# Two hT blocks per load and an earlier preparation of the last group, in a gated graph layer on one core

## The chip, the cores and the metric

The kernel runs on one core of one Trainium2 chip. The metric is the device time of one execution in microseconds. Four executions of the kernel before took 1185.64 to 1194.97 us, median 1188.67.

## What is computed

For 16 graphs (batch b) of 1024 nodes with 256 features x, with one sparse weighted adjacency matrix `adj` (1024 x 1024, shared by the batch):

```
pre_u  = x @ W1[:256]             pre_v = x @ W1[256:]
S[u,v] = sigmoid( sum_k relu(pre_u[u,k] + pre_v[v,k] + b1[k]) * W2[k] + b2 )
a[v]   = sum_u S[u,v] * adj[u,v] * x[u]
m[v]   = (sum_u adj[u,v] * x[u]) * x[v]
out    = beta1*x + beta2*(a @ Wa + ba) + beta3*(m @ Wm + bm)
```

S matters only where adj is not zero, so the kernel works on lists of edges.

## The kernel before

**Units of work.** The batch is cut into `NG` = 4 groups of `GB` = 4 graphs, the nodes v into `NT` = 8 blocks of 128. A pair (group, node block) is one unit `k`, 32 in all, in the sequence `order` (L381): group 0 blocks 0 to 5, group 1 blocks 0 to 5, group 0 blocks 6 and 7, group 1 blocks 6 and 7 (these last four are `again`, L382), then groups 2 and 3 whole. A unit takes 10 steps (`T`), so there are 320 steps; step `n` belongs to unit `n // 10` and has a place `s = n % 10` in it. Below, "block 180" means steps 180 to 189. The main loop is L700 to L778. Every engine works through its instructions in the order in which the program writes them (`manual_schedule`, L444), so the order is written out by hand.

**One step.** GpSimd gathers (L469, `fetch`) 128 rows of 8 KB, 1 MB, from a table in DRAM: each row holds pre_u and x of one neighbour u for the four graphs. There are five buffers, and the gather for step n + 4 is issued in step n, after the aggregation of step n - 1 has freed its buffer. VectorE adds pre_v to the gathered pre_u (L555, one instruction, "the gating add"), then does relu, times W2 and the sum for each graph (L559, four times). ScalarE takes the sigmoid (L562) and scales the left operand (L565). TensorE aggregates (L576) in the step after and spreads pre_v for the step after next to the edges (`expand`, L539), into one of two PSUM buffers.

**Beside the steps, by s.** At s = 0 and 2 TensorE computes pre_v of the next unit (`halves`, L425; w_v in L400). At s = 1, 7, 9 results are transposed (L594). At s = 3 to 6 `block_end` multiplies by Wa and Wm (L625) for the unit before; its result z leaves by a 512 KB store (L631), and at s = 0 the block of x that goes into it is loaded (h_blk, L730), both on SP's queue. VectorE multiplies by x in `times_h` (L607), which reads hT; for the second half of unit k that is at step 10k + 13, and then hT of the unit is dropped (L609). In steps 0 to 107 the edge lists of node blocks 4 to 7 are made as well (`advance`, L675), with GpSimd fetching two columns of edge values per step.

**Preparing the tables.** Each table row block needs two things: a copy of x from DRAM to DRAM (`copy_h`, L392, 512 KB, on ScalarE's queue in the main loop), and pre_u, computed from hT, the transposed x block of 128 partitions x 8 x 128 numbers (`load_hT`, L386: 512 KB, in runs of 512 bytes, on SP's queue). `rows` (L407) computes pre_u in two pieces of 8 matmuls (w_u in L400), each copied out by ScalarE (L416); one step after the second piece the result is stored in the table (L419) by SP. All of a group's table must be in place before its first gather, which is issued four steps ahead of the group's first step: steps 56, 156 and 236 for groups 1, 2 and 3. hT is read again by `halves` and by `times_h` when the unit itself is processed. For the four units in `again` it is dropped after `rows` and loaded a second time.

**When.** Group 0 is prepared ahead of the main loop ("the lead"; the order is the script at L488, the loads are at L478 to L483). For the others, `plan` (L681) gives each block the step of its load and copy and the steps of its two row pieces (L687 to L692). Each load is put at the end of its step (L765).

**Buffers.** The pool `hts` (L213) has NT + 2 = 10 buffers of one block each, `hta` (L214) three for the `again` units. A load into a buffer waits, on SP's queue, until the last reader of the block that had the buffer before is done. The last unit's output rows use one more tile of `hts` (L732).

Of the kernel before, what the change touches and what calls it, by code (L numbers as in the profile page):

```python
# [7 lines left out]
FP = mybir.dt.float32  # L8
# [5 lines left out]
P = 128  # L14
# [3 lines left out]
def kernel(  # L18
# [42 lines left out]
    nc = tc.nc  # L61
    B, N, D = x.shape
    NT = N // P
    DC = D // P
    GB = 4
    NG = B // GB
# [20 lines left out]
    xT_rows = xT.rearrange("b (c p) n -> p (b c) n", p=P)  # L87
# [121 lines left out]
    main = ctx.enter_context(ExitStack())  # L209
    gat = main.enter_context(tc.tile_pool(name="gat", bufs=1))  # L210
    one = main.enter_context(tc.tile_pool(name="one", bufs=1))
    big = main.enter_context(tc.tile_pool(name="big", bufs=2))
    hts = main.enter_context(tc.tile_pool(name="hts", bufs=NT + 2))  # L213
    hta = main.enter_context(tc.tile_pool(name="hta", bufs=3))  # L214
    wk = main.enter_context(tc.tile_pool(name="wk", bufs=3))
    psc = main.enter_context(tc.tile_pool(name="psc", bufs=2, space=bass.MemoryType.PSUM))
# [157 lines left out]
    def after(step, f):  # L374
        due.setdefault(step, []).append(f)
# [5 lines left out]
    order = [(g, vt) for some in (range(FIRST), range(FIRST, NT)) for g in range(2) for vt in some]  # L381
    again = [(g, vt) for g, vt in order if vt >= FIRST]  # L382
    order += [(g, vt) for g in range(2, NG) for vt in range(NT)]
    hTs = {}

    def load_hT(k):  # L386
        g, nt = k
        hTs[k] = hta.tile([P, GB, DC, P], FP, name="hT_") if k in again else hts.tile([P, GB, DC, P], FP, name="hT")
        nc.sync.dma_start(hTs[k].rearrange("p b c n -> p (b c) n"),
                          xT_rows[:, g * GB * DC:(g + 1) * GB * DC, nt * P:(nt + 1) * P])  # L390

    def copy_h(k, engine=nc.scalar):  # L392
        g, nt = k
# [53 lines left out]
    def do(step):  # L447
        for f in due.pop(step, ()):
            f()
# [10 lines left out]
    BS = NG * NT  # L460
# [15 lines left out]
    turn = [(g, vt) for g in range(2) for vt in (*range(FIRST, NT), *range(FIRST))]  # L476
    tabs = [fetched[0][:, :GD], *(f[:, GD:] for f in fetched)]
    for i in range(NT):  # L478
        if i < 2:
            next(made[i])  # L480
        load_hT(turn[i])
        if i in (5, 7):
            next(made[i // 2])  # L483
    COPIES = 2
# [5 lines left out]
    m = 0  # L490
# [76 lines left out]
    def aggregate(n):  # L567
        k, g, vt, w, j = where(n)
        left, f = lefts.pop(n), fetched[n % NF]
        for i, q in enumerate(QUARTERS[j]):  # L570
            h, r = divmod(q, 2)
            first = j == h * MID and r == 0
            if first:
                accs[h] = psa.tile([P, 2, D], FP, name=f"acc{h}")
            for b in range(GB):
                nc.tensor.matmul(accs[h][b * 2 * V:(b + 1) * 2 * V, r, :],  # L576
                                 left[:, i, b].rearrange("p k v -> p (k v)"), f[:, GD + b * D:GD + (b + 1) * D],
                                 start=first, stop=(j == q + 1), skip_group_check=True)


    def half_end(n, q):

        evs[q] = one.tile([P, 2, D], FP, name=f"ev{q}")
        nc.scalar.copy(evs[q], accs.pop(q))  # L584
# [94 lines left out]
    loads, at = {}, {}  # L679

    def plan(blocks, ns):  # L681

        for k, (load, *pieces) in zip(blocks, ns):
            loads[load] = k
            at.update((n, k) for n in pieces)

    plan(turn[NT:], ((0, 5, 8), (6, 12, 15), (12, 18, 22), (17, 25, 28), (24, 32, 35), (31, 38, 42), (38, 45, 48),  # L687
                     (43, 50, 52)))
    plan([(2, vt) for vt in range(NT)], ((60 + 10 * i, 68 + 10 * i, 71 + 10 * i) for i in range(NT)))
    plan([(3, vt) for vt in range(NT)], ((141, 149, 151), (149, 158, 161), *((153 + 10 * i, 161 + 10 * i, 168 + 10 * i)  # L690
                                                                             for i in range(2, NT - 1)), (223, 231, 234)))
    plan(again, ((103,), (113,), (125,), (133,)))  # L692
    begun = set(turn[:NT])
    end = parts = piece = last = None
    load_mark(0)
    for n in range(2):
# [3 lines left out]
    for n in range(total + 2):  # L700
        k, s = divmod(n, T)
        if 1 <= n <= total:
            aggregate(n - 1)
            fetch_val(2)
            if n - 1 + NF < total:
                fetch(n - 1 + NF)
            if n % TW in (0, MID + 1):
                half_end(n - 1, 0 if n % TW else 1)
        if n < total:
            gate(n)  # L710
            if n + 1 < total:
                left_adj(n + 1)
        if n % TW == 1 and n // TW + 1 < total // TW:
            load_mark(n // TW + 1)
        do(n)
        if n + 2 < total:
            expand(n + 2)
        if n == 1:
            w_a = load_weights(Wa, "w_a", nc.sync)
            w_m = load_weights(Wm, "w_m", nc.sync)  # L720
            bias = load_rows(bm, D, "bias", nc.sync)
            ba_b = load_rows(ba, D, "ba_b", nc.sync)
            be1 = load_rows(beta1, 1, "be1", nc.sync)
            be2 = load_rows(beta2, 1, "be2", nc.sync)
            be3 = load_rows(beta3, 1, "be3", nc.sync)
            after(10, scale_late)
        if s == 0 and 0 < k < BS:
            hbs[k - 1] = big.tile([P, GB, D], FP, name="h_blk", bufs=1)
            g, vt = order[k - 1]
            nc.sync.dma_start(hbs[k - 1], x_rows[vt * P:(vt + 1) * P, g * GB:(g + 1) * GB, :])  # L730
        if n == total - 6:
            hbs[BS - 1] = hts.tile([P, GB, DC, P], FP, name="hT").rearrange("p b c n -> p b (c n)")  # L732
            for v, m, f in tails:
                for h, o in tail_rows(x, v, m, f):
                    nc.sync.dma_start(h, o)
        for i in advance.get(n, ()):
            next(made[i], None)
        if (s == 1 and 0 < k < BS) or n == total:
            turn_over(k - 1, 1, 1, n)
        if s in (3, 4, 5, 6) and 0 < k < BS:  # L740
            if s == 3:
                end = block_end(k - 1)
                next(end)
            go(end, n)
        if s == 7 and k < BS:
            turn_over(k, 0, 0, n)
            turn_over(k, 0, 1, n)
# [12 lines left out]
        if k + 1 < BS and s in (0, 2, 3, 5, 6):  # L760
            if s == 0:
                parts = halves(k + 1)
                next(parts)
            go(parts, n)
        if n in loads:  # L765
            load_hT(loads[n])
            if loads[n] not in begun:
                copy_h(loads[n])
                begun.add(loads[n])
        if n in at:  # L770
            if at[n] != last:
                last = at[n]
                piece = rows(last)
                next(piece)
            go(piece, n)
        if n == 100:
            nc.gpsimd.partition_all_reduce(longest, rest, P, bass_isa.ReduceOp.max)
            after(n + 12, count_rest)  # L778
# [7 lines left out]
    with tc.If(any_left > 0):  # L786
        with ExitStack() as s2:
# [3 lines left out]
            for vt in range(NT):  # L791
# [3 lines left out]
                for b in range(B):  # L795
                    hT = fw.tile([P, DC, P], FP, name="fb_hT")
# [96 lines left out]
```

## Time and profile before

| | us |
|---|---|
| median of four runs | 1188.67 |
| the profiled execution, its own time | 1181.59 |
| its span, first to last instruction | 1179.7 |
| first gating add (step 0) starts at | 71.16 |
| first gating add of group 1 (step 60) | 310.7 |
| first gating add of group 2 (step 160) | 653.8 |
| first gating add of group 3 (step 240) | 909.6 |
| last gating add (step 319) | 1159.1 |

The profile is of one execution. In it "PE" is TensorE's matmuls and "PEld" its weight loads, which overlap them, DVE is VectorE, ACT ScalarE, POOL GpSimd, SP SyncE, whose only work is to issue DMAs. A matmul's end is modelled, so a PE that is busy all the time is not PE at its peak. "A <- B" in a list of waits means that A stood idle until B ended; "remote" is a release that the profile can't attribute. The trace also has a record of every DMA packet: queue q0 is GpSimd's, q1 is SP's, q10 is ScalarE's. A share of 1.00 is 16 DMA engines busy; since packets overlap, up to 1.17 is seen in the lead.

### The profile page before, as it was taken

Reading aid. Unit: us, or ns where it says so; the run is one execution under the profiler, and the core shown is the slowest. Engines: PE = TensorE matmul, PEld = TensorE weight load, DVE = VectorE, ACT = ScalarE, POOL = GpSimd, SP = SyncE. Lnnn points to the kernel's source line nnn. Section 1 sums busy time; section 2 is a strip of 40 time slices with the busy share of each in tenths; the row PEclk is TensorE's granted clock in tenths of the full one; section 3 lists DMA queues with packets and bytes.
Section 4 is the critical chain, followed back from the end, with each engine's and each line's share of the span. In section 5 each row is a group of like instructions: output and inputs, shape, how many; then the busy total and the mean of one; then the engine's idle time right before and its main releaser. Section 6 shows DMA issues by size and latency. Waiting matters only on the chain. (4 is left out here: it accounts for less than half of the span.)

```text
span 1179.7 us, 23919 instructions
## 1 busy us (share of the span) xinstructions
PE 1095.8 (93%) x7633; PEld 726.6 (62%) x7633; DVE 1063.1 (90%) x3487; ACT 893.5 (76%) x2624; POOL 437.5 (37%) x428
## 2 busy tenths in 40 slices
PE   7767899999799999999999999999999999999986
PEld 6644566666566666566666666666666566666653
DVE  7678789979998999899999999999999999999994
ACT  2437577778678886788887888888888888888873
POOL 1546663343253332633332333333333333333330
PEclk9968999999999999999999999999999999999999
DMA  9987799999989998999999999999999999999992
GB/s 283 303 284 237 254 339 372 315 318 383 319 268 350 366 382 302 308 379 380 385 380 364 363 354 350 370 371 366 380 358 341 351 319 323 329 332 335 325 352 82
DMA packets 147047, 391.40 MB, mean 332 GB/s; under 512 B 16752, under 2 KB 105328, under 8 KB 110704
## 3 DMA queue, kind: packets, MB, share of 16 engines
q0 software_dynamic: 50016, 300.50, 69.7%
q1 hardware_dynamic: 81616, 74.99, 19.7%
q10 hardware_dynamic: 15280, 14.29, 3.7%
q8 instruction: 63, 1.03, 0.3%
q14 instruction: 72, 0.59, 0.1%
HBM read 393.78 MB, written 50.33 MB: 376 GB/s over the span
## 5 line engine op out<-in xcount | busy, mean ns | idle before, releaser
L469 POOL DMA_INDIRECT fetched<-table,uidx x320 | 340.3, 1064 | 647.8 <-PE acc L576 498.1
L559 DVE SCALAR_TENSOR_TENSOR t<-t,w_b 128x256 f32<-128x256 f32 x1280 | 469.6, 422 | 22.5 <-ACT left L565 0.5
L555 DVE TENSOR_TENSOR t<-fetched,pc 128x1024 f32<-128x1024 f32 x320 | 389.4, 1217 | 47.3 <-DMA fetched<-table,uidx 17.9
L576 PE MATMUL acc<-fetched,left 128*32 128x256 f32 x4096 | 340.4, 391 | 36.3 <-ACT left L565 24.4
L565 ACT ACTIVATE left<-left,gt 128x32 f32<-128x32 f32 (+1 forms) x1280 | 299.3, 304 | 10.4
L539 PE MATMUL pc<-X,mark 128*128 128x512 f32 x640 | 236.9, 452 | 13.8 <-DVE t L555 8.9
L576 PEld LDWEIGHTS acc<-fetched,left 128*32 128x32 f32 x4096 | 134.7, 109 | 184.4 <-issue 56.6
L539 PEld LDWEIGHTS pc<-X,mark 128*128 128x128 f32 x640 | 96.8, 190 | 147.6 <-issue 78.8
L562 ACT ACTIVATE gt<-sc,b_b 128x4 f32<-128x4 f32 x320 | 96.2, 301 | 74.0 <-DVE t L559 68.8
L625 PE MATMUL misc<-w_m,LT 128*128 128x256 f32 x496 | 117.2, 379 | 0.0
L625 PE MATMUL misc<-w_a,LT 128*128 128x256 f32 x496 | 117.1, 379 | 0.0
L549 ACT ACTIVATE left<-onehot,val 128x128 f32<-128x128 bf16 (+1 forms) x320 | 116.5, 364 | 0.0
L400 PE MATMUL misc<-w_u,hT 128*128 128x256 f32 x448 | 107.8, 387 | 5.1 <-ACT few L310 3.6
L400 PE MATMUL misc<-w_v,hT 128*128 128x256 f32 x448 | 108.8, 387 | 0.0
L559 DVE DVE_READ_ACCUMULATOR t<-t,w_b 128x1 f32 x1280 | 104.4, 82 | 0.0
L625 PEld LDWEIGHTS misc<-w_a,LT 128*128 128x128 f32 x496 | 93.9, 189 | 15.0
L625 PEld LDWEIGHTS misc<-w_m,LT 128*128 128x128 f32 x496 | 93.9, 189 | 15.0
L357 POOL DMA_INDIRECT val<-in_adjT_dram,vidx x80 | 84.4, 1055 | 32.7 <-issue 23.6
L400 PEld LDWEIGHTS misc<-w_v,hT 128*128 128x128 f32 x448 | 87.3, 195 | 14.4
L400 PEld LDWEIGHTS misc<-w_u,hT 128*128 128x128 f32 x448 | 84.8, 193 | 16.9 <-ACT few L310 3.7
L597 ACT COPY LT<-misc 128x512 f32<-128x512 f32 x128 | 70.2, 573 | 19.3 <-PE pc L539 7.6
L584 ACT COPY ev<-acc 128x512 f32<-128x512 f32 x128 | 75.6, 591 | 11.0 <-PE acc L576 3.7
(161 smaller groups left out, 895.1 us busy)
## 6 DMA issues: line engine op xcount, KB each, us to landing
h_blk<-in_x_dram SPq DMA_DIRECT2D x31, 512.0 KB
out_dram<-z SPq DMA_DIRECT2D x31, 512.0 KB
hT<-in_xT_dram SPq DMA_DIRECT2D x28, 512.0 KB
table<-tab SPq DMA_DIRECT2D x26, 512.0 KB
table<-in_x_dram ACTq DMA_DIRECT2D x24, 512.0 KB
fetched<-table,uidx POOLq DMA_INDIRECT x320
table<-in_x_dram SPq DMA_DIRECT2D x8, 512.0 KB
table<-fetched SPq DMA_DIRECT2D x6, 512.0 KB
```

The source lines that it names most:

```text
L357: nc.gpsimd.indirect_dma_start(out=val[:, i, j:j + 1], out_offset=None, in_=adj_flat, in_offset=bass.IndirectOffsetOnAxis(ap=vidx[:, i, j: ...
L400: nc.tensor.matmul(p[:, bb * D:(bb + 1) * D], hT[:, 2 * h + bb, i, :], wt[:, i, :], start=(i == 0 and not begun), stop=(i == DC - 1), skip ...
L469: nc.gpsimd.indirect_dma_start(out=fetched[n % NF], out_offset=None, in_=table[g], in_offset=bass.IndirectOffsetOnAxis(ap=uidx[:, vt * NW ...
L539: nc.tensor.matmul(pcs[n][:, c], marks[n // TW][:, j * P:(j + 1) * P], cuts[k][:, w, c], start=True, stop=True)
L549: nc.scalar.activation(lefts[n][:, :m, :, 0, :], onehot[:, i, o:o + m, :].unsqueeze(2).to_broadcast([P, m, GB, V]), AF.Copy, scale=val[:, ...
L555: nc.vector.tensor_tensor(t, fetched[n % NF][:, :GD].rearrange("p (b d) -> p b d", b=GB), pcs.pop(n).rearrange("p (b d) -> p b d", b=GB), ...
L559: nc.vector.scalar_tensor_tensor(t[:, b, :], t[:, b, :], 0.0, w2_b, ALU.max, ALU.mult, accum_out=sc[:, b:b + 1])
L562: nc.scalar.activation(gt, sc, AF.Sigmoid, bias=b2_b)
L565: nc.scalar.activation(lefts[n][:, :m, b, 1, :], lefts[n][:, :m, b, 0, :], AF.Copy, scale=gt[:, b:b + 1])
L576: nc.tensor.matmul(accs[h][b * 2 * V:(b + 1) * 2 * V, r, :], left[:, i, b].rearrange("p k v -> p (k v)"), f[:, GD + b * D:GD + (b + 1) * D ...
L584: nc.scalar.copy(evs[q], accs.pop(q))
L625: nc.tensor.matmul(pz[:, bb * D:(bb + 1) * D], LTs[k][:, c, 2 * h + bb, i, :], wt[:, c, :], start=False, stop=(i == 0 and c == DC - 1), sk ...
```

## The change

`load_hT` loads two neighbouring node blocks of a group at once into one tile of twice the width, so that the runs are 1024 bytes; `hts` has 5 such tiles in place of 10 single ones. The call for the second block of a pair then finds it there and loads nothing. Blocks 2, 3 and 4 of group 3 (`alone`) are loaded by themselves into `hta`, as are the four loads of `again`; block 7 of group 3 has no partner left and goes alone into a wide tile. The very first pair is loaded as two halves (`apart`). The steps in `plan` are new for groups 1 to 3, the copy is issued ahead of the load in a step, and the last output tile comes from `hta`.

```diff
-    hts = main.enter_context(tc.tile_pool(name="hts", bufs=NT + 2))
+    hts = main.enter_context(tc.tile_pool(name="hts", bufs=NT // 2 + 1))
...
-    def load_hT(k):
+    alone = [(NG - 1, vt) for vt in range(2, 5)]
+    def load_hT(k, apart=False):
         g, nt = k
-        hTs[k] = hta.tile([P, GB, DC, P], FP, name="hT_") if k in again else hts.tile([P, GB, DC, P], FP, name="hT")
-        nc.sync.dma_start(hTs[k].rearrange("p b c n -> p (b c) n"),
-                          xT_rows[:, g * GB * DC:(g + 1) * GB * DC, nt * P:(nt + 1) * P])
+        blocks = [k]
+        if k in begun or k in alone:
+            t = hta.tile([P, GB, DC, P], FP, name="hT_")
+        else:
+            t = hts.tile([P, GB, DC, 2 * P], FP, name="hT")
+            if nt + 1 < NT:
+                blocks.append((g, nt + 1))
+        n = P * len(blocks)
+        for c in range(0, n, P) if apart else (0,):
+            m = P if apart else n
+            nc.sync.dma_start(t.rearrange("p b c n -> p (b c) n")[:, :, c:c + m],
+                              xT_rows[:, g * GB * DC:(g + 1) * GB * DC, nt * P + c:nt * P + c + m])
+        for i, k in enumerate(blocks):
+            hTs[k] = t[:, :, :, i * P:(i + 1) * P]
+            begun.add(k)
...
-        load_hT(turn[i])
+        if i % 2 == 0:
+            load_hT(turn[i], i == 0)
...
-    plan(turn[NT:], ((0, 5, 8), (6, 12, 15), (12, 18, 22), (17, 25, 28), (24, 32, 35), (31, 38, 42), (38, 45, 48),
-                     (43, 50, 52)))
-    plan([(2, vt) for vt in range(NT)], ((60 + 10 * i, 68 + 10 * i, 71 + 10 * i) for i in range(NT)))
-    plan([(3, vt) for vt in range(NT)], ((141, 149, 151), (149, 158, 161), *((153 + 10 * i, 161 + 10 * i, 168 + 10 * i)
-                                                                             for i in range(2, NT - 1)), (223, 231, 234)))
+    plan(turn[NT:], ((0, 8, 11), (5, 12, 15), (7, 18, 21), (12, 23, 25), (24, 32, 35), (31, 38, 41), (44, 51, 52),
+                     (46, 53, 54)))
+    plan([(2, vt) for vt in range(NT)], ((64, 72, 73), *((60 + 10 * i, 68 + 10 * i, 71 + 10 * i) for i in range(1, NT))))
+    plan([(3, vt) for vt in range(NT)], ((131, 148, 151), (139, 158, 161), (158, 168, 171), (163, 178, 181),
+                                         (170, 188, 191), (183, 194, 198), (188, 202, 208), (203, 214, 218)))
...
-            hbs[BS - 1] = hts.tile([P, GB, DC, P], FP, name="hT").rearrange("p b c n -> p b (c n)")
+            hbs[BS - 1] = hta.tile([P, GB, DC, P], FP, name="hT_").rearrange("p b c n -> p b (c n)")
...
         if n in loads:
-            load_hT(loads[n])
-            if loads[n] not in begun:
+            if loads[n] not in copied:
                 copy_h(loads[n])
-                begun.add(loads[n])
+                copied.add(loads[n])
+            if loads[n] not in hTs:
+                load_hT(loads[n])
```

`turn[NT:]` is group 1 in the sequence of blocks 6, 7, 0, 1, 2, 3, 4, 5. With the pairs, group 1 is loaded in steps 0, 7, 24, 44, group 2 in 64, 80, 100, 120, group 3 in 131, 158, 163, 170, 183, 203.

More of the change, by code (lines that the diff above doesn't have):

```diff
@@ L383 @@
     order += [(g, vt) for g in range(2, NG) for vt in range(NT)]
-    hTs = {}
-    def load_hT(k):
+    hTs, begun = {}, set()
+    alone = [(NG - 1, vt) for vt in range(2, 5)]
+    def load_hT(k, apart=False):
         g, nt = k
-        hTs[k] = hta.tile([P, GB, DC, P], FP, name="hT_") if k in again else hts.tile([P, GB, DC, P], FP, name="hT")
-        nc.sync.dma_start(hTs[k].rearrange("p b c n -> p (b c) n"),
-                          xT_rows[:, g * GB * DC:(g + 1) * GB * DC, nt * P:(nt + 1) * P])
+        blocks = [k]
[13 more added lines that the diff above has]
+            begun.add(k)
     def copy_h(k, engine=nc.scalar):
@@ L685, in plan @@
             at.update((n, k) for n in pieces)
-    plan(turn[NT:], ((0, 5, 8), (6, 12, 15), (12, 18, 22), (17, 25, 28), (24, 32, 35), (31, 38, 42), (38, 45, 48),
-                     (43, 50, 52)))
-    plan([(2, vt) for vt in range(NT)], ((60 + 10 * i, 68 + 10 * i, 71 + 10 * i) for i in range(NT)))
-    plan([(3, vt) for vt in range(NT)], ((141, 149, 151), (149, 158, 161), *((153 + 10 * i, 161 + 10 * i, 168 + 10 * i)
-                                                                             for i in range(2, NT - 1)), (223, 231, 234)))
+    plan(turn[NT:], ((0, 8, 11), (5, 12, 15), (7, 18, 21), (12, 23, 25), (24, 32, 35), (31, 38, 41), (44, 51, 52),
[3 more added lines that the diff above has]
+                                         (170, 188, 191), (183, 194, 198), (188, 202, 208), (203, 214, 218)))
     plan(again, ((103,), (113,), (125,), (133,)))
-    begun = set(turn[:NT])
+    copied = set(turn[:NT])
     end = parts = piece = last = None
```

## Prediction

> **What bounds the kernel now.** I read the page first (shares by engine, DMA by slice), then the busy time block by block (ten steps each, cut at the start of every tenth gating add, L555), then what the VectorE waits for, then the DMA packets of three short windows.
>
> ```profile
> PE 1095.8 (93%) x7633; PEld 726.6 (62%) x7633; DVE 1063.1 (90%) x3487; ACT 893.5 (76%) x2624; POOL 437.5 (37%) x428
> ...
> DMA  9987799999989998999999999999999999999992
> ```
>
> TensorE, VectorE and the DMA engines are all near full, so no single row names the bound; the blocks do. Columns: stretch, length, then busy us (and instructions) of PE, PEld, DVE, ACT, POOL, clock, DMA share, GB/s.
>
> ```profile
> 232.30:272.00 39.70, 37.35 (x260) 24.73 (x259) 30.36 (x97) 28.86 (x85) 18.64 (x20) 1.00 0.93 339
> 346.90:382.80 35.90, 33.32 (x230) 21.93 (x229) 30.31 (x96) 28.03 (x84) 15.36 (x16) 1.00 0.99 349
> 717.40:748.80 31.40, 31.40 (x229) 20.86 (x227) 30.25 (x97) 26.85 (x81) 10.16 (x10) 1.00 0.98 344
> 780.70:813.50 32.80, 32.80 (x242) 21.60 (x235) 30.21 (x97) 27.84 (x84) 11.72 (x11) 1.00 1.00 371
> 877.10:909.60 32.50, 31.94 (x229) 21.32 (x229) 30.25 (x97) 27.34 (x81) 11.26 (x10) 1.00 0.94 346
> 909.60:942.50 32.90, 31.78 (x233) 20.13 (x225) 30.26 (x97) 26.64 (x81) 11.11 (x11) 1.00 0.98 360
> 973.80:1005.10 31.30, 30.15 (x217) 19.20 (x216) 30.15 (x97) 26.32 (x80) 10.50 (x11) 1.00 0.91 326
> ```
>
> The last line is a block of the last group (steps 260 to 269), with nothing prepared beside it: VectorE works 30.15 us of 31.30. That is the floor of a block. Blocks 180, 200 and 230 (third to fifth line) carry two row pieces each: PE is busy nearly all the time and DMA is at 0.94 to 1.00, three limits within a few per cent of each other. Block 240 has no pieces and is still 1.6 us over. The first two lines (steps 40 to 49, 70 to 79) have the same VectorE work and are 4.6 to 8.4 us longer: these are real stalls. Their causes, VectorE alone, steps 0 to 79 and then 80 to 249:
>
> ```profile
> DVE t L555 <- DMA fetched<-table,uidx: 6.7, 4, 2.8
> DVE t L555 <- PE pc L539: 6.5, 4, 2.0
> DVE t L555 <- remote: 6.0, 4, 2.4
> ```
>
> ```profile
> DVE t L555 <- DMA fetched<-table,uidx: 10.1, 17, 1.5
> DVE t L555 <- PE pc L539: 3.9, 6, 1.1
> ```
>
> In all some 19 us early and 14 us later are waits for a gather or for PE. A change that only moves loads and pieces can't win more, and can lose by adding to them.
>
> **What the Trainium skill says.** (1) "DMA: Bandwidth & Descriptors", section "Why small descriptors are slow (HBM only)": each packet carries a fixed overhead. The trace agrees. In three windows (12 to 18 us: only hT loads, 512 B packets; 62 to 72 us: 8 KB gathers beside hT; 973.8 to 1005.1 us: 1 KB packets of h_blk and z):
>
> ```profile
> q1 hardware_dynamic: 3440, 1.74, 116.2%
> ```
>
> ```profile
> q0 software_dynamic: 570, 3.89, 93.6%
> q1 hardware_dynamic: 526, 0.26, 9.0%
> ```
>
> ```profile
> q1 hardware_dynamic: 1014, 1.00, 9.4%
> ```
>
> Share x window x 16 / packets gives 32.4 ns and 27.4 ns for 512 B, 46.5 ns for 1 KB. (2) Same page, "Queues, rings and completion order": each DMA engine takes turns between queues packet by packet. The second window agrees: 570 gather packets beside 526 hT packets. So a gather of 8 KB packets keeps most of an engine, and a burst on SP's queue delays gathers modestly but for long. (3) Same page, "Issuing engines are not separate DMA queues": that copy_h stays on ACT's queue doesn't take it out of the same sum.
>
> **The change, part by part.**
>
> *Pairs.* 32 first loads become 13 pair loads and 6 singles (the first pair is sent as two). A pair costs 1024 x 46.5/16 = 2.98 us of DMA time against 2048 x 27.4/16 = 3.51 (or 4.15 at 32.4 ns): 0.5 to 1.2 us less, 0.7 taken, as the mean of all 36,864 packets of 512 B in the trace is 29 ns. 13 x 0.7 = 9 us of DMA time, most of it where DMA doesn't set the end. Matmuls (L400) and the product (L607) have the same shapes: nothing. SP issues 13 loads fewer; worth nothing, as SP mostly waits. The same SBUF is used (5 x 8 KB against 10 x 4 KB a partition).
>
> *Lead (0 to 71 us).* Three pairs save 2 us of DMA before the copies. But the first gating add waits for PE at 71.16, behind the list chain of VectorE that ended in ACT few L310 at 68.5, not for a gather (the first is issued at 56.2). Cover: that chain. Value 0; range -1.7 (all of it shows) to +1 (blocks 0 and 1 of group 0 land together: first used at 17.3 us, and their 1 MB is in by about 15 by the packet count).
>
> *Steps 0 to 79.* Loads of group 1 and 2 move from 0, 6, 12, 17, 24, 31, 38, 43, 60, 70 to 0, 7, 24, 44, 64, so none lies on step 70 any more, where h_blk, z, a copy and hT met and the gather of step 74 was 2.81 us late: -2.0 taken, 0 to -2.8. Each new wait is for a pair buffer; by the code its last reader is the product L607 of step 23, 43, 63, one step ahead of the load on SP, and what is queued behind the load is later work. Price 0. Row pieces at 42 and 45 go (to 41, 51): the one at 42 ran right behind w_v and put the aggregation off:
>
> ```profile
> 243.97 1.89 PE L400 MATMUL misc<-w_v,hT 128*128 128x256 f32 x8
> 245.70 1.89 PE L400 MATMUL misc<-w_u,hT 128*128 128x256 f32 x8
> 247.52 1.07 PE L576 MATMUL acc<-fetched,left 128*32 128x256 f32 x16
> 249.47 1.22 DVE L555 TENSOR_TENSOR t<-fetched,pc 128x1024 f32<-128x1024 f32 x1 [2.00 <-PE pc L539]
> ```
>
> Gates 44 and 45 stood 2.00 and 1.25 us for PE: -2.0 taken, 0 to -3.3. Gates 23 and 41 (2.32 and 2.42, releaser not told) each fell where an hT load met z and h_blk; both loads are gone: -1.0 taken, 0 to -4.7. On the other side four pieces now sit on steps 51, 52, 53, 54 in a row (before: 45, 48, 50, 52), and two on 72, 73 (before 68, 71). I price these by PE's lag. From the starts of PE's groups in steps 260 to 269 a step needs, from s=0 on, 3.3, 1.8, 3.7, 3.7, 3.4, 3.2, 3.0, 2.6, 1.6, 2.1 us (28.3 a block), a piece 1.83 more, VectorE allows 3.13 a step (3.6 where lists run). Without pieces the lag peaks at 1.4 us and nothing waits; pieces at 32, 35, 38 reached 3.1 and nothing waited. So 1.4 to 3 us of lag is free. Steps 51 to 54 reach 5.4: +2.4 to +4.0, 2.4 taken. Steps 72, 73 reach 5.0: +2.0 to +3.6, against the 1.8 us that gates 71 and 73 lose to PE now: +0.5 taken. ACT, which empties these pieces, is 76% busy and covers its 0.59 us copies; if not, they are in that range. The last table store of group 1 moves from step 53 to 55, one step ahead of the first gather of that group (issued in step 56) on POOL. If it lands late, that gather and those behind it wait up to one step, 3 us; gather 60 was issued at 296.1 and used at 310.7, so 14.6 us hide it: 0. Sum: -2.0 - 2.0 - 1.0 + 2.4 + 0.5 = -2.1.
>
> *Steps 80 to 249, transfers.* Five pairs here save 3.5 us of DMA time, and 10.1 us of gates wait for gathers, mostly three steps after a load met h_blk: -1.8, as half reaches the end (0 to -3.5). Against it pair 131, two copies and again-load 133 meet within four steps: 3.0, 2 x 1.5 (512 packets of 46.5 ns), 1.9 and 3.0 for h_blk with z, 10.9 us against 8.3 now; gate 133 already waited 0.80: +1.0 (0 to +2.5). Net -0.8.
>
> *Rows of the last group.* Eight blocks are 16 pieces either way. Blocks 160, 170, 190 get 1, 2 and 1 more; 220 and 230 lose 2 each. With two pieces a block PE needs 28.3 + 3.7 = 32.0, with three 33.8. Blocks 160 and 170 took 32.0 and 31.7: +0.5. Blocks 190 to 219 have seven pieces, 84.9 + 12.8 = 97.7, against 96.2 measured with six, and pieces at s=4 and s=2 lie badly: +1.8. Blocks 220, 230, 240 took 97.4 and should come near the floor, 94.3: -3.1. Net -0.8. The first gather of group 3 no longer follows a fresh store (897.9, gather 902.1). Last tail buffer from the other pool: free since step 273, 0.
>
> **Sum.** 0 - 2.1 - 0.8 - 0.8 = -3.7 us. The profiled execution took 1181.59 us (span 1179.7, 1.9 around it) and would become 1177.9. It is 0.6% under the median shown, so I put the same difference on the median: 1188.67 - 3.7 = 1185.0.
>
> **Rivals.** *Transfers were the bound.* The DMA share of 1.00 speaks for it, PE at 100% in the same blocks against it. Then pairs bring most of their 7 us outside the lead, gates 23, 41 and 74 run clear (a further -3), and PE's stacking hides: about -10, 1179. *PE stacking decides* (the slower side). Place: steps 51 to 54, 72 and 73, 191 to 218. If PE's free lag is only 1.4 us, it costs 4.0 + 3.1 (after what gates 71 and 73 lose now, with some carried over) + 3; the gathers wait for the aggregation, so each lag also shifts the next fetch: about +2. If the early stalls then come back as other waits, nothing is against it but -3.1: +9, 1197. It decides once the free lag is under about 2 us. For it: gate 44 lost 2.00 us with a lag near 3. Against: steps 32 to 38. *Hidden anyway*: gains and losses inside each other's slack, 1189; the queue does hold the pairs, so the transfers themselves can't fail to change.
>
> **How the numbers follow.** Forecast 1185.0: 0.30. Hidden: 0.12. Transfers: 0.27. Stacking: 0.31. An effect under 0.5% (5.9 us) is about what a measurement of this kernel can't tell from no change. Faster 0.27, same 0.42, slower 0.31. Range: the open costs sum to about -12 and +11 us, trimmed where both ends need every term at once: 1177 to 1199.
>
> **What would show it.** Right: the 512 B packets of hT fall from 36,864 to 10,240 (10 loads: the first pair's two, four singles, four loaded again); blocks 220 to 249 together within 1 us of 94.3; no 2 us gates at 44 and 74; gaps for PE at 53 to 56 of 2 to 4 us; blocks 190 to 219 near 98. Wrong: SP's pair loads waiting with a z or a table store stuck behind; gather 60 waiting for its store with the DMA idle; lead longer than 72 us; gathers late at every step 83, 103, 123.

## The result and the profile after

The changed kernel takes 1193.11 us (median of 42 runs, 1183.90 to 1201.43) against 1188.80 us for the kernel before (63 runs beside it). The ratio is 1.0038, 95% interval [1.0026, 1.0050]: 4.5 us slower, where 3.7 us faster was forecast. Repeated on two more occasions, beside the kernel before each time (runs g1_after and z2_after), it gave 1.0028 [1.0008, 1.0048] and 1.0028 [1.0017, 1.0038]. The profiled execution took 1189.17 us (span 1187.3).

First the page: shares of engines, DMA by slice, SP's queue (packets, MB, share).

```profile
PE 1098.0 (92%) x7633; PEld 727.5 (61%) x7633; DVE 1063.3 (90%) x3487; ACT 894.6 (75%) x2624; POOL 440.9 (37%) x428
...
DMA  9896799799988999899999999999999999999993
...
q1 hardware_dynamic: 68096, 74.98, 18.7%
```

The work is the same: every engine's busy time is within 0.8% of before. SP's queue moves the same 74.98 MB in 68,096 packets; before they were 81,616, with a share of 19.7%. So the pairs do what they say: the hT packets of 512 B are down to 10,240. The time that they save doesn't show. The blocks that were shown of before (steps 40, 70, 180, 200, 230), same columns:

```profile
233.90:272.90 39.00, 34.88 (x245) 22.19 (x243) 30.21 (x97) 27.83 (x83) 18.77 (x20) 0.96 0.92 333
347.30:385.10 37.80, 33.14 (x219) 22.53 (x219) 30.33 (x96) 25.78 (x76) 14.42 (x15) 0.95 0.84 288
724.50:756.90 32.40, 32.40 (x235) 21.50 (x234) 30.20 (x97) 27.35 (x82) 11.30 (x11) 1.00 0.98 367
788.30:822.50 34.20, 34.16 (x250) 22.57 (x252) 30.26 (x96) 28.55 (x86) 10.15 (x11) 1.00 1.01 374
887.70:919.00 31.30, 30.07 (x214) 19.07 (x213) 30.15 (x96) 26.34 (x80) 9.97 (x11) 1.00 0.92 327
```

Block 230 stands on VectorE's floor, as wanted, 1.2 us shorter. Block 200 is 1.4 us longer, block 180 1.0, block 70 1.9. In the changed kernel the gating add is at L571 (L555 before), the products with w_v and w_u at L415, the aggregation at L592, the gather at L484 and the load of hT at L401. What VectorE waits for in steps 80 to 249:

```profile
DVE t L571 <- DMA fetched<-table,uidx: 19.1, 17, 3.6
DVE t L571 <- PE pc L555: 1.6, 2, 1.0
```

The waits of the gating add for PE fell from 3.9 to 1.6 us, those for gathers rose from 10.1 to 19.1: as many waits, longer ones.

One profile of before against one of after is not enough here: runs of one kernel spread by some 10 us, and the first profile of before lay 7 us under its median. So both were profiled once more, side by side (runs z1_before and z2_after; before takes 1169.4 us there). Their stages are steps 0 to 79, 80 to 129, 130 to 189 and 190 to 249; first before, then after:

```profile
71.70:372.20 300.50, 279.16 (x1896) 186.15 (x1896) 276.01 (x925) 224.30 (x656) 148.13 (x143) 0.97 0.91 323
372.20:544.50 172.30, 166.46 (x1178) 110.24 (x1176) 161.74 (x530) 139.16 (x410) 63.74 (x62) 0.99 0.98 356
544.50:737.10 192.60, 189.87 (x1368) 124.51 (x1368) 181.21 (x572) 162.43 (x483) 62.96 (x60) 1.00 1.00 363
737.10:930.70 193.60, 191.85 (x1390) 126.02 (x1382) 181.20 (x572) 164.62 (x487) 64.66 (x61) 1.00 0.99 364
```

```profile
71.70:370.60 298.90, 278.49 (x1882) 185.59 (x1885) 276.24 (x924) 223.78 (x653) 149.76 (x143) 0.97 0.90 323
370.60:545.50 174.90, 167.27 (x1197) 110.85 (x1197) 161.90 (x529) 139.64 (x412) 65.30 (x63) 1.00 0.98 359
545.50:740.00 194.50, 193.21 (x1398) 127.80 (x1395) 181.21 (x571) 164.40 (x489) 65.36 (x61) 1.00 1.00 376
740.00:936.60 196.60, 191.94 (x1355) 125.25 (x1353) 181.24 (x571) 161.99 (x481) 64.66 (x61) 1.00 0.94 338
```

The difference is -1.6, +2.6, +1.9 and +3.0 us, then -1.7 in what follows step 250: +4.2 together, as the spans (1168.1 and 1172.3). Between the first two profiles the same stages differ by +1.9, +3.4, +2.4, +0.2 and -0.7. So a single pair of profiles doesn't say which stage loses. One stretch is alike in both pairs: steps 190 to 229 took 128.4 and 128.5 us in the two profiles of before, 130.8 and 132.0 in those of after. In z1_before and z2_after:

```profile
737.10:865.50 128.40, 128.40 (x937) 84.94 (x930) 120.65 (x381) 110.39 (x327) 40.84 (x40) 1.00 1.00 370
```

```profile
740.00:872.00 132.00, 130.35 (x923) 85.89 (x921) 120.88 (x381) 109.28 (x323) 41.84 (x41) 1.00 0.95 343
```

VectorE does the same work in 3.6 us more, with the DMA at 0.95 where it was at 1.00, and PE, busy all the time before, now stands at times. The extra time is waiting, and the lists of waits below say for what.

### The profile page after: what moved, and what is told of

The parts are those of the page before. It is cut to its first block, busy times and chain, and to the rows that moved or that the text cites. A ratio compares the mean times of both kernels' runs of the same rounds, so it can differ in the third digit from the quotient of the medians.

```text
span 1187.3 us, 23897 instructions
## 1 busy us (share of the span) xinstructions
PE 1098.0 (92%) x7633; PEld 727.5 (61%) x7633; DVE 1063.3 (90%) x3487; ACT 894.6 (75%) x2624; POOL 440.9 (37%) x428
## 3 DMA queue, kind: packets, MB, share of 16 engines
q1 hardware_dynamic: 68096, 74.98, 18.7%
q8 instruction: 63, 1.03, 0.3%
## 5 line engine op out<-in xcount | busy, mean ns | idle before, releaser
L484 POOL DMA_INDIRECT fetched<-table,uidx x320 | 344.4, 1076 | 652.3 <-PE acc L592 501.4
L571 DVE TENSOR_TENSOR t<-fetched,pc 128x1024 f32<-128x1024 f32 x320 | 389.4, 1217 | 58.8 <-DMA fetched<-table,uidx 26.4
L592 PE MATMUL acc<-fetched,left 128*32 128x256 f32 x4096 | 341.2, 390 | 38.4 <-ACT left L581 28.1
L555 PE MATMUL pc<-X,mark 128*128 128x512 f32 x640 | 237.1, 452 | 15.8 <-DVE t L571 10.7
L592 PEld LDWEIGHTS acc<-fetched,left 128*32 128x32 f32 x4096 | 134.4, 109 | 187.6 <-ACT left L581 60.5
L555 PEld LDWEIGHTS pc<-X,mark 128*128 128x128 f32 x640 | 96.8, 190 | 149.8 <-issue 79.6
L415 PE MATMUL misc<-w_u,hT 128*128 128x256 f32 x464 | 116.8, 401 | 17.3 <-ACT LT L613 6.1
L415 PEld LDWEIGHTS misc<-w_u,hT 128*128 128x128 f32 x464 | 91.5, 201 | 31.6 <-ACT LT L613 6.5
L415 PE MATMUL misc<-w_v,hT 128*128 128x256 f32 x400 | 96.0, 383 | 0.0
L415 PEld LDWEIGHTS misc<-w_v,hT 128*128 128x128 f32 x400 | 76.9, 192 | 12.3
```

Of the source, the lines that this page charges most:

```text
L415: nc.tensor.matmul(p[:, bb * D:(bb + 1) * D], hT[:, 2 * h + bb, i, :], wt[:, i, :], start=(i == 0 and not begun), stop=(i == DC - 1), skip ...
L484: nc.gpsimd.indirect_dma_start(out=fetched[n % NF], out_offset=None, in_=table[g], in_offset=bass.IndirectOffsetOnAxis(ap=uidx[:, vt * NW ...
L555: nc.tensor.matmul(pcs[n][:, c], marks[n // TW][:, j * P:(j + 1) * P], cuts[k][:, w, c], start=True, stop=True)
L571: nc.vector.tensor_tensor(t, fetched[n % NF][:, :GD].rearrange("p (b d) -> p b d", b=GB), pcs.pop(n).rearrange("p (b d) -> p b d", b=GB), ...
L592: nc.tensor.matmul(accs[h][b * 2 * V:(b + 1) * 2 * V, r, :], left[:, i, b].rearrange("p k v -> p (k v)"), f[:, GD + b * D:GD + (b + 1) * D ...
```

## The experiments

All ratios are against the kernel before, run beside it on the same chip; runs measured side by side are a set. Before takes about 1189 us beside the runs whose names begin with e, g and h, and 1169 beside those with f, k and z, so only ratios are compared across these. The kernel before against itself gave 0.9999 [0.9986, 1.0012] (z1_before).

### Which part of the change loses

Theory at this point: the last group's rows. Rivals: the pair loads as bursts, or the steps of groups 1 and 2.

*e1_rows*: before, and of the change only the last group's plan.

```diff
-    plan([(3, vt) ...], ((141, 149, 151), (149, 158, 161), ... (223, 231, 234)))
+    plan([(3, vt) ...], ((131, 148, 151), (139, 158, 161), (158, 168, 171), (163, 178, 181),
+                         (170, 188, 191), (183, 194, 198), (188, 202, 208), (203, 214, 218)))
```

> The kernel before with one part of the change alone: the last group's loads and row pieces in the new steps (131 to 218), blocks 2 to 4 of it in the three-buffer pool, every hT still loaded singly. Rows theory (the new steps of the last group crowd TensorE and the transfers in steps 131 to 218): 3 to 5 us slower than before, with blocks 190 to 219 together 1.5 us or more longer and nothing changed ahead of step 130. Burst theory (a pair load leaves SP right behind z and h_blk and the gathers arrive late): within 2 us of before, since no pair is loaded. My prediction's term for this part was -0.8 us.

Measured 1194.72 us, 1.0044 [1.0022, 1.0065], 5.2 us: all of the loss without one pair load. Blocks 190 to 219 took 98.8 us in its profile, 96.2 in the first of before.

*e2_old_rows*: the changed kernel with that plan taken back.

> The changed kernel with the last group's loads and pieces put back into the old steps (141 to 234); pairs and the steps of groups 1 and 2 stay. Rows theory: the loss of 4.5 us is gone, within 1 us of before. Burst and stacking theories: 3 to 6 us slower than before remain, in blocks 70 and 80 above all (5.0 us there between the two traces).

Measured 1188.36, 0.9987 [0.9967, 1.0007]: nothing is left of the loss.

*e3_behind*: the changed kernel with three pair loads of group 2 three or four steps later, behind the table store.

```diff
-  (60 + 10 * i, ...) for i in range(1, NT)
+  (60 + 10 * i + (0, 0, 3, 0, 4, 0, 3, 0)[i], ...) for i in range(1, NT)
```

> The changed kernel with the pair loads of group 2 in steps 83, 104 and 123 in place of 80, 100 and 120, so that in SP's sequence they stand behind the table store of the block and no longer right behind z and h_blk. Burst theory: the gather of step 81 is no longer 3.65 us late, blocks 80 to 129 together are 2 to 4 us shorter, the whole 0.5 to 2.5 us slower than before. Stacking theory (row pieces on heavy steps, 72 and 73 above all): no change from the changed kernel, 4 to 5 us slower than before.

Measured 1202.45, 1.0092 [1.0057, 1.0127]: slower still, so the remedy was wrong, and neither theory had forecast it. The trace shows one place: the pair load of step 123 left SP at 543.9, and the first product that reads it got it at 570.8, 27 us later. PE stood for 6.64 us, and the gate behind it (step 131) for 6.7:

```profile
570.81 3.75 PE L415 MATMUL misc<-w_u,hT 128*128 128x256 f32 x8 [6.64 <-DMA hT<-in_xT_dram]
```

*e6_five*: the changed kernel with the steps of all groups as before, so that only the pairs and their five buffers are left.

> The changed kernel with all steps of all groups as in the kernel before: pair loads into the five wide buffers at the step at which the first block of a pair was loaded before (blocks 2 to 4 of the last group still alone). Stacking and rows theories: the cause is gone, 0 to 4 us faster than before for the shorter transfers. Burst theory: every pair still leaves with z and h_blk, 2 to 5 us slower than before. Late gathers at steps 10k+1 to 10k+4 of the blocks with a pair load and none at the others would show the bursts.

Measured 1188.22, 0.9991 [0.9970, 1.0012]: the pairs alone make no difference, over the whole kernel, that this interval can tell.

### Early loads or late pieces

Two parts of the last group's plan are suspects: its first two loads go from 141 and 149 to 131 and 139, and the last six pieces go to 194, 198, 202, 208, 214 and 218, of which three lie at s=4 and s=2 of their block. The other loads and pieces move up as well, in every kernel below with new pieces, the spaced ones included.

*f1_e1_141*: e1_rows with the first two loads at 141 and 149.

> The kernel of the run e1_rows (before, with the last group's new steps, single loads), but its first two loads back at steps 141 and 149 as before, in place of 131 and 139; all pieces and the other loads stay new. Theory 'late pieces' (pieces at s=4, 8 and 2 in steps 194 to 218 put the aggregation back, so the gathers of five steps later leave late and gates 203, 213 and 223 wait): still 1193 to 1195, +4 to +6 over before. Theory 'early loads' (loads at 131 and 139 crowd SP's queue round the again-load of step 133, and gates 133 to 146 wait): back to 1188 to 1190. If both carry, about 1191 to 1192.

Measured 1171.35, 1.0031 [1.0017, 1.0046].

*f2_b_131*: before with only these loads at 131 and 139.

> The kernel before with only the first two loads (and copies) of the last group moved from steps 141 and 149 to 131 and 139; all pieces as before. 'Early loads': 1192 to 1194. 'Late pieces': 1188 to 1190, no change.

Measured 1173.23, 1.0049 [1.0032, 1.0066].

*f3_198*: the changed kernel with spaced pieces, one at s=8 and one at s=1.

```diff
- (183, 194, 198), (188, 202, 208), (203, 214, 218)
+ (183, 198, 201), (188, 208, 211), (203, 218, 221)
```

> The changed kernel with the last six pieces at steps 198, 201, 208, 211, 218, 221 (s=8 and s=1) in place of 194, 198, 202, 208, 214, 218 (s=4, 8, 2, 8, 4, 8); all loads stay. 'Late pieces': the issue-to-gate lead of gathers 199 to 203 goes back from about 7 to about 9 us, gate 203 waits under 1 us in place of 2.3, and the time is 1188 to 1190 or below. 'Early loads': no change, 1192 to 1194.

Measured 1168.37, 0.9994 [0.9979, 1.0010]. Repeated later:

> The run f3_198 once more, beside the others. If the early load's cost depends on the chip's speed: 1.001 to 1.003 here on a chip where before takes 1188 us, 0.999 on one where it takes 1169. If spaced pieces alone remove the loss: 0.999 to 1.000.

Measured 1169.41, 1.0017 [1.0001, 1.0034]. The two differ more than the theory says, in sets where the kernel before takes the same 1169 us, so the dependence on the chip's speed wasn't tested. The same kernel moved by 0.23% from one set to another: differences of about 0.2% between separate sets tell little.

*f4_a_141*: the changed kernel with the loads at 141 and 149.

> The changed kernel with the first two loads of the last group (one pair load and two copies) back at steps 141 and 149. 'Early loads': 1188 to 1190. 'Late pieces': no change, 1192 to 1194.

Measured 1170.74, 1.0019 [1.0003, 1.0034].

So neither theory stood alone: both parts cost, each without the other, and by the middle values the two costs don't add (f2_b_131 and f1_e1_141 together would make 0.8%, e1_rows has 0.44%).

### How the late pieces cost

A gather is issued four steps ahead of its gate, once the aggregation of the step before has freed its buffer: gather 199 follows the aggregation of step 194. In z2_after the piece of step 194 runs on PE ahead of the aggregation, and the gather of step 199 (POOL) waits for that:

```profile
757.97 1.89 PE L415 MATMUL misc<-w_u,hT 128*128 128x256 f32 x8
759.79 0.64 PE L592 MATMUL acc<-fetched,left 128*32 128x256 f32 x8
```

```profile
760.81 1.21 POOL L484 DMA_INDIRECT fetched<-table,uidx  x1 [3.77 <-PE acc L592]
...
773.83 1.00 POOL L484 DMA_INDIRECT fetched<-table,uidx  x1 [2.24 <-PE acc L592]
```

The bracket is the idle time of GpSimd ahead of the gather. In z1_before that gap is 2.04 us for gather 199, not 3.77. The time from a gather's issue to the moment its gate would run if the data were there (its lead) follows from the two streams, in us:

```
gather  z1_before  z2_after  f3_198  before  after
199        8.8       7.6       9.0     9.1    7.4
201        8.3       7.0       8.5     8.5    6.8
203        7.5       6.3       7.7     8.1    6.1
gate 203
 waits     1.4       2.0       0.1     1.2    2.2
```

The other profiles agree. Over the seven with the changed pieces the lead of gather 199 is 7.3 to 7.9 us and gate 203 waits 2.0 to 3.8; over the eight with the old pieces these are 8.8 to 10.5 and 0.2 to 1.9, over the four with spaced pieces 9.0 to 9.5 and 0.1 to 0.8.

The lead that one piece takes away (1.7 us by the two gaps) isn't won back in the four steps that follow: gathers and gates go on at the same pace, and only the wait at gate 203 restores it. Gather 203 was issued at 773.83 (second line above) and its gate ran at 782.08, 8.3 us later; before it was 769.77 and 778.70, 8.9 us. So gather 203, issued at s=9 and used at s=3, took over 8 us where its gate waited, though one came within 7.8 in f3_198. There was little or no free lag: before already waited there. After it, gates 212, 213 and 223 wait 1.5, 1.3 and 1.3 us in z2_after, the second of them for PE. VectorE's waits for gathers in steps 190 to 249, for z1_before, z2_after and f3_198:

```profile
DVE t L555 <- DMA fetched<-table,uidx: 4.7, 6, 1.4
```

```profile
DVE t L571 <- DMA fetched<-table,uidx: 7.1, 7, 2.0
```

```profile
DVE t L571 <- DMA fetched<-table,uidx: 3.3, 8, 1.0
```

The stage took 193.6, 196.6 and 190.9 us. The pair kernels with spaced pieces give 190.9 to 191.5 there (f3_198, k3_198, g2_both), those with the changed pieces 193.8 to 196.6. The old pieces give 193.3 to 195.0: over the whole stage the changed pieces cost little against them, as there are three pieces fewer, and the loss hides behind that gain. Steps 190 to 229 show it alone (from the starts of the gating adds, in us; k2_194, which is mixed, is left out):

```
                               pieces there   steps 190-229
8 profiles, old pieces               8        127.9 to 129.1, mean 128.6
7 profiles, changed pieces           7        130.7 to 132.0, mean 131.2
4 profiles, spaced pieces            7        126.6 to 127.7, mean 127.0
```

The three ranges don't touch, with pairs or with single loads. With the same seven pieces the changed places take 4.2 us more than the spaced ones, so it is the place of the pieces and not their number. f3_198's line for these steps:

```profile
739.20:866.20 127.00, 126.44 (x919) 83.42 (x916) 120.70 (x382) 108.53 (x324) 40.26 (x40) 1.00 0.96 349
```

*k2_194*: only 194 and 198 become 198 and 201.

> The changed kernel with only the pieces of steps 194 and 198 moved to 198 and 201; 202, 208, 214, 218 and all loads stay. If the piece at s=4 is most of the late-piece loss: gate 203 waits under 1 us, about 2 us less than the changed kernel (1.001 to 1.002). If all three blocks carry it: 1.002 to 1.004, gates 213 and 223 wait as in the changed kernel.

Measured 1170.61, 1.0029 [1.0014, 1.0043]. Gate 203 no longer waits, but 206, 207 and 223 do (0.7, 1.2, 2.0 us), the stage is at 194.4 and steps 190 to 229 at 130.5. So the piece at s=4 isn't most of the loss; the pieces left in their places carry most of it.

*k4_rows*: before, with single loads, the last group's loads from 141 on and the spaced pieces.

> The kernel before (single loads) with the last group's loads and pieces at ((141, 148, 151), (149, 158, 161), (158, 168, 171), (163, 178, 181), (170, 188, 191), (183, 198, 201), (188, 208, 211), (203, 218, 221)): the rows done two blocks earlier than before, but one piece at s=8 and one at s=1 in each block, and no load ahead of the again-load. 'Two placements explain the loss': 0.997 to 0.999 of before. If earlier rows cost by themselves: 1.002 or more.

Measured 1167.75, 0.9993 [0.9978, 1.0008]: the loss is gone, but the gain that was expected isn't shown. Against f1_e1_141, which differs in the six pieces alone, that is 0.38% or 4.4 us by the ratios. Its one trace doesn't put that in one stage: 193.4 us in steps 190 to 249 against 193.7, and 192.7 in steps 130 to 189 against 194.9. In steps 190 to 229 it is 127.7 against 131.0.

### How the early loads cost

*g1_after* repeats the changed kernel, *g2_both* has both remedies (pieces of f3_198, loads at 141 and 149):

> The changed kernel itself, so that its ratio stands on the chip of the other three: 1.003 to 1.005 of before.

> The changed kernel with the last six pieces at 198, 201, 208, 211, 218, 221 and the loads of blocks 0 and 1 of the last group at 141 and 149. If late pieces are the loss and early loads add a little: 0.996 to 0.999 of before. If the pieces alone are the loss, the same as the run f3_198: 0.999 to 1.000.

Measured 1193.83, 1.0028 [1.0008, 1.0048], and 1189.47, 0.9993 [0.9971, 1.0016]. So g2_both stands where f3_198 does: beside spaced pieces, taking the early loads away as well brings nothing that these intervals can tell. *h1_pair131* and *h2_apart131* put only the early loads on the kernel of e2_old_rows, as one pair load or as two:

> The changed kernel with the last group's old steps (the run e2_old_rows), but its first pair load and two copies at 131 and 139. Theory 'full queue' (SP's own issue stalls, for up to 8 us, when too many packets stand in its queue; a pair has 1024 packets for two blocks in place of 2048, so it stays short): 0.998 to 1.001 of before, and no issue of SP above 4 us near that step. Rival 'bytes' (the extra megabyte beside the again-load is the cost): 1.003 to 1.005.

> The run h1_pair131 with that one pair load sent as two loads of 512 B packets: same bytes, same step, 2048 packets in place of 1024. 'Full queue': 1.003 to 1.005 of before, the table store after it stalls SP for 5 to 8 us and a product waits for the again-load. 'Bytes': same as h1_pair131.

Measured 1193.25, 1.0038 [1.0020, 1.0056], and 1196.79, 1.0056 [1.0037, 1.0076]. So "full queue" fails as the main cause: the pair, with SP never stalled, costs nearly as much; the 0.18% between the two lie inside their intervals. The trace of g1_after shows another victim:

```profile
601.95 2.72 PE L415 MATMUL misc<-w_v,hT__6418 128*128 128x256 f32 x8 [2.21 <-DMA hT__6418<-in_xT_dram]
```

This is the block loaded again at step 133, first read at step 141. It waits in SP's queue behind z, h_blk and the megabyte of the pair. Read from issues, last packet and first matmul of that tile, in us:

```
kernel       load of group 3   issued   last packet   first read   PE waits
g1_after     131, ahead        577.9      601.4         601.9        2.2
z2_after     131, ahead        557.6      580.6         581.4        0.9
k2_194       131, ahead        555.4      579.3         579.9        2.0
h1_pair131   131, ahead        578.5      600.1         601.1        -
g2_both      141, behind       583.0      591.3         605.1        -
f4_a_141     141, behind       556.7      565.0         578.9        -
k1_pair134   134, behind       558.2      566.5         580.4        -
```

It takes 22 to 24 us to its last packet in one case and 8 in the other: 14 us of slack become 0.5 to 1.0. In g1_after the gathers behind that product leave late, and gate 151 waits 3.19 us. Not every profile shows such a wait. With the load at 131 PE stood 0.4 to 2.9 us for the again-load in seven of ten (e3_behind apart), and not at all in the first profile of the changed kernel, in k3_198 and in h1_pair131. Steps 130 to 159 took 96.0 to 101.7 us in these ten (mean 98.2) and 95.8 to 98.7 in the nine others (mean 96.8).

*k1_pair134*: h1_pair131 with pair and copy at 134, so that the order on SP's queue is swapped, and the bytes stay. The pair also leaves 14 us later, no longer right behind z and h_blk.

```diff
- (131, 149, 151)
+ (134, 149, 151)
```

> The run h1_pair131 (last group's old pieces, pair load and copy at 131) with that pair load and copy at step 134, so that it goes behind the again-load of step 133 on SP's queue: the same bytes within 10 us. 'Again-load late': the again-load lands more than 8 us ahead of its product, and the time is 0.998 to 1.001 of before. 'Bytes': 1.003 to 1.005, as h1_pair131.

Measured 1170.88, 1.0013 [0.9999, 1.0027]: by the middle values two thirds of the cost of h1_pair131 are gone, its interval ends below what "bytes" expected, and the again-load lands 14 us ahead of its use. It isn't all gone for certain: the ratio lies just above what "again-load late" expected. Nor does the run separate the again-load from a rival, that the pair right behind z and h_blk makes the gathers of steps 131 to 139 late: gates there waited 2.0 us in h1_pair131 and 0.6 in k1_pair134, while PE didn't wait for the again-load in either. And the two runs come from different sets, which alone can differ by 0.2%. That the order decides when the again-load lands is shown (8 us against 22); how much of the time it costs, and through whom, is in part open. f2_b_131 with single loads (PE 2.0 us for the again-load, then gates 145, 146 and 156 waiting 0.9, 1.6 and 1.2) has more than one effect in it.

The last two runs give the stages shown above:

> The kernel before against itself: 0.998 to 1.002. Its blocks 80 to 129 tell whether the 174.6 us of the first profile were luck: about 178 if so, as every run on such a chip with the new or the old steps showed 178 to 181.

> The changed kernel once more beside it: 1.003 to 1.004. If early loads and late pieces are the loss, it is longer than z1_before mainly in steps 130 to 159 and in 200 to 229, by 2 to 3 us each.

Measured 1169.52, 0.9999, and 1172.60, 1.0028 [1.0017, 1.0038]. Blocks 80 to 129 took 172.3 us in z1_before, but in a set at 1169 us, so this run doesn't answer for the others. There e1_rows, which is the kernel before up to step 130, took 179.3 us: the 174.6 of the first profile may well have been luck. The second expectation was half right: steps 200 to 229 grew by 3.7 us, but 130 to 159 by 0.7 only, and 80 to 129 by 2.6.

## Why the prediction was wrong, point by point

*What bounds the kernel.* Right in kind: VectorE's floor, and gathers that come late. The share of the DMA said little about either. PE's sum says more, as steps 190 to 229 show below.

*Pairs.* Packets as predicted. "9 us of DMA time" may be so, but their place was wrong. Ten profiles from the sets in which before takes 1169 us:

```
us                     steps 80-129              250 to the end
4 kernels, singles     171.4 to 172.8, mean 172.2   236.7 to 237.6, mean 237.3
6 kernels, pairs       173.1 to 175.5, mean 174.4   235.4 to 237.0, mean 236.2
```

Steps 80 to 129 became 2.2 us longer, where "-1.8" stood for the transfers of steps 80 to 249, and the end 1.1 us shorter. All six pair kernels also have the new steps of groups 1 and 2, so these profiles don't part the two. By e6_five and e2_old_rows it comes to about zero over the whole (0.9991 and 0.9987); the gain of some 4 us that the prediction had outside the last group lies at the edge of their intervals. That a pair, z and h_blk leave SP as one burst of 2 MB and hold up gates 82 and 114 fits the traces; it wasn't isolated, since e3_behind moved the loads too near their use. I priced a load at its step. SP runs ahead of the steps: with no wait in front of it the load goes right behind z.

*Lead.* 0 predicted, 0.0 measured between z1_before and z2_after (71.7 both).

*Steps 0 to 79.* -2.1 predicted, -1.6 side by side; but the means of the ten profiles are 299.4 and 299.7, so I can't claim it. The terms were not right one by one: gates 45 and 74 still wait 2.8 and 2.3 us in z2_after, both for gathers, and no gate stands at 53 to 56, where 2.4 us of stacking were priced.

*Steps 80 to 249, transfers.* +1.0 for the crowd at 131 to 134, range to 2.5: the direction was right. Steps 130 to 159 grew by 0.7 us side by side and by 1.4 on average over the profiles with the load at 131; by the runs with the old pieces the early loads cost 0.25% (h1_pair131 less k1_pair134) to 0.5% (f2_b_131), 3 to 6 us. What I missed is the again-load behind the pair: I priced the bytes and not the order on the queue.

*Rows of the last group.* This is the step that failed most. For the whole plan of the last group the prediction had +0.2 us (+1.0 for the crowd, -0.8 for the rows); alone, in e1_rows, it cost 0.44%, 5.2 us. The new places of the rows without the early loads cost 0.31%, 3.6 us, in f1_e1_141. Of "-0.8", -1.3 stood for steps 190 to 249: +1.8 for blocks 190 to 219 and -3.1 for blocks 220 to 249. Means over the seven profiles with the changed pieces and the eight with the old ones:

```
blocks       old    changed   measured   predicted
190 to 219   96.4    98.5       +2.0       +1.8
220 to 249   97.5    96.1       -1.5       -3.1
```

"Blocks 190 to 219 near 98" held within the spread (97.9 to 99.4). What didn't come is the gain behind them: blocks 220 to 249 took 95.8 and 97.2 us in the two profiles of after, not 94.3. Block 220, with no piece left in it, still took 32.7 us on average over the seven, and in each of them gate 223 waited 1.1 to 2.0 us for its gather. Blocks 160 to 189, priced at +0.5, grew by 1.1. Against the spaced places the pieces cost 0.26% (f4_a_141 to g2_both) to 0.38% (f1_e1_141 to k4_rows), 3 to 4.5 us by the ratios and 4.2 us in steps 190 to 229. The prediction's own sum for PE (28.3 us a block, 1.83 a piece) shows what it left out. For steps 190 to 229 it gives 127.8 us with the old pieces and 126.0 with the changed or the spaced ones; the means are 128.6, 131.2 and 127.0. The sum holds to about 1 us where the gathers keep their lead, and misses 5 where they lose it. The failed premise is "1.4 to 3 us of lag is free". I measured PE's lag against the gate that VectorE runs next; the shortest slack was that of the gather which the aggregation releases for five steps later, and at s=3 it was at or below zero already (gate 203 waited 1.2 and 1.4 us in the two profiles of before). The rival "PE stacking decides" had this place, this chain ("each lag also shifts the next fetch") and the point from which it decides; 0.31 was too little for it, though its +9 us was too much. With the spaced pieces the gain does come, in the pair kernels: 190.9 us in place of 193.6 is -2.7 (f3_198). With single loads it is 193.4 (k4_rows), so what the pairs add there is open.

*Still open*: why the costs of early loads and late pieces don't add; why early loads cost 0.4 to 0.5% beside the old pieces (h1_pair131, f2_b_131) and next to nothing beside the spaced ones (f3_198 and k3_198 against g2_both); and what, beyond the again-load, f2_b_131 loses.

None of the kernels tried beats the kernel before by more than its interval; e2_old_rows, g2_both and k4_rows are level with it.

## What to carry to other kernels

When work is moved on an engine, price it against the prefetch that this engine releases: read the time from a transfer's issue to its use, compare it with what the transfer takes in that place, and treat only the rest as free. Here such a lead was lost at once and came back only through a wait, so put extra work where the lead is longest, in portions that a step can take. And when a load is moved ahead on a queue, look at the next load behind it that has a fixed time of use.

## What the runs showed of the hardware that was not expected

An issue on SP mostly takes 0.3 to 1.4 us in these traces, but some took several times as long. In f2_b_131, with z, h_blk and two single loads in a row (3072 packets), SP's issues were (start, duration):

```profile
538.98 6.13 SPq L389 DMA_DIRECT2D hT<-in_xT_dram  x2
549.90 8.42 SPq L419 DMA_DIRECT2D table<-tab  x1
558.43 0.40 SPq L389 DMA_DIRECT2D hT__6441<-in_xT_dram  x1
```

h2_apart131 shows 8.45 and 8.78 us in the same place; h1_pair131, with the same bytes in 2048 packets, has none over 2 us in the whole main loop. So the larger packets kept SP free there, though the kernel wasn't shown to be shorter for it.

The same load took 8 us from issue to its last packet in k1_pair134 and 22 in h1_pair131, which differ in the order on SP's queue and not in the bytes. The DMA share doesn't tell the two apart: it was 1.04 during the 8 us of g2_both and 1.03 during the 24 us of g1_after. What differs is what stands ahead of the load in its own queue, beside the gathers.

My reading that a gather keeps most of a DMA engine fits the pair of e3_behind (27 us), but not bursts. In the profile of after, between 383 and 393 us, in each microsecond in which SP's queue started 160 to 312 of its 1 KB packets the gathers started 4 to 27 of their 8 KB packets, in place of some 40 to 50. One for one, as in the prediction's second window (570 beside 526), they don't alternate there. In what portions an engine takes its turns no run here shows.
